# Two graph layers on one core: head and tail written in another order, filler matmuls at more places, and another address for one small tile

## The chip, the cores and the metric

The kernel runs on one core of a Trainium2 chip. The metric is the device time of one execution in microseconds (us), lower being better. The core has five engines that run side by side and wait for each other through semaphores: TensorE (PE in the profile; PEld is its loading of weights), VectorE (DVE), ScalarE (ACT), GpSimd (POOL) and SyncE (SP), which here only starts DMA transfers. The clock of TensorE can be granted in full or in part, and the profile shows which share it had.

## The reference

There are 128 graphs of 128 nodes with 512 features, and one adjacency matrix for each. Every graph goes through two layers, each of which normalises its input, applies relu, does a graph operation and adds the input back:

```python
h = jnp.maximum(_layernorm(x, axis=-1), 0.0)
x = x + _L0_gnn_ref(h, adj, W1, b1, gamma, beta, W2, b2)
h = jnp.maximum(_layernorm(x, axis=-1), 0.0)
x = x + _L1_gnn_ref(h, adj, W)
```

The first graph operation is a hypergraph convolution, relu, a layer norm over 1024 channels, a second convolution and a residual. The second takes the mean over neighbours and a linear layer of the features beside that mean:

```python
def hypergraph_conv(x, adj, W, b):
    H = (adj != 0).astype(x.dtype)
    w = adj.reshape(N, -1)[:, :C]
    xw = jnp.einsum('ncd,hd->nch', x, W)
    Dn = 1 / jnp.einsum('nce,ne->nc', H, w)
    Be = 1 / H.sum(axis=1)
    m = Be[:, :, None] * jnp.einsum('nce,nch->neh', H, xw)
    return Dn[:, :, None] * jnp.einsum('nce,neh->nch', H, m) + b
# layer 1
agg = jnp.einsum('bij,bjf->bif', adj, x) / jnp.maximum(deg, EPS)
out = relu(jnp.einsum('bnf,of->bno', jnp.concatenate([x, agg], 2), W))
```

## The kernel before

One tile is one graph: 128 nodes on the 128 partitions. The work on a graph is cut into some seventy small stages, each a Python function with the graph's number as argument (`x_sums`, `incidence`, `conv1_weights` and so on), and the order in which the stages are called is the order of the instructions on every engine. No planner chooses it: it is written by hand in three lists. `head` starts graphs 0 to 4 and prepares the weights, `step(s)` is repeated for s = 3 to 124 and holds stages of five or six graphs at different depths, and `tail` finishes the last seven, called y, z, a, b, c, d, e. A stage that was already called for a graph is skipped. `step` is not touched by the change.

Large products are done in a reduced-precision form of fp32 with both operands split into a high part h, a low part l and a combined part d. `product` (L440 to L463) runs h with h and l with l into one PSUM bank (L455; rm, gm, bm, am) and d with d into another (L460; rd, gd, bd, ad). So each weight needs three tiles: `Half.high` on ACT (L173), `Half.low` on DVE (L177), and `Half.rest`, which is one DVE operation (L189), four POOL operations (L80), or four matmuls with the tile `unit`, which holds two signed identities, and copies on ACT (L193 to L195, tile wd). Small products are full fp32: ps_s (L375, the node matrix s from the adjacency), pz (L413, features times s) and py (L628).

For one graph the stages run as follows.

- `load_adjb` brings the adjacency in 32 x 32 blocks (four DMAs of small pieces, two buffers), `incidence` turns and counts it on DVE (L361 to L369), `node_matrix` multiplies it and copies s on ACT (L377), and `node_scale` computes the scale dinv on DVE.
- `x_sums`, `x_spread`, `scales` and `x_norm` are the first norm: ACT sums with accumulators (L294 to L300), two small DVE operations (L305, L306), and ACT again (L310).
- `conv1_nodes` is pz, `conv1_high`, `conv1_low` and `conv1_rest` split it into z (ACT L426, DVE L430 and L433), `conv1_weights` is the product with one half of W1, `conv1_main` and `conv1_out` take it out of PSUM (ACT L475, DVE L480), and `conv1_bias` adds b1.
- `inner_sums` to `inner_norm` normalise the 1024 channels. `inner_out` and `inner_in` send r to DRAM and bring it back in blocks (n_scratch, nb, on SP), `inner_turn` turns the blocks on DVE (L516), and `inner_high`, `inner_low` and `inner_rest` make nh, nl and nd (L537, L80, L546).
- `conv2_weights` is the product gm/gd, `conv2_weights_out` and `conv2_bias` make g (L619, and L80 with the tile c), `conv2_nodes` is py, and `conv2_out` adds to x (L632). `residual` adds the first norm's output and b2 to x on POOL.
- The second layer has its own norm (`layer1_sums` to `layer1_norm`), trip through DRAM (h_scratch, hb), turn and split (hh, hl, hd), a product bm/bd whose result is split again (bh, bl, bd), and a product am/ad.
- `mean_operator`, `mean_out`, `mean_in`, `mean_transpose` and `mean_rest` divide the adjacency by its degree, turn it through DRAM (an_scratch, anb) and make the three parts `anp` (ACT L344, DVE L347 and L348). `aggregate` multiplies them with bh, bl and bd into the open banks am and ad (L710: three matmuls per graph), and `finish` writes the output.

Weights of these matmuls are loaded from the tile named last in a row such as `am<-bh,anp`: there anp is the loaded operand and bh the streamed one.

Two devices matter for the change. First, `fill(columns)` puts matmuls of a constant on the next PSUM bank that is asked for (L94), whose result nobody reads. In fp32 a filler of 512 columns is two matmul instructions, each 0.43 us at full clock and 0.85 at half clock in this trace. The last filler added to the list is issued first. Second, the address of a pool's tile follows from the order in which tags are first used: a tag that is first used later lies behind. `unit` (L202 to L209) borrows the tags anp and ant, so the call of `unit()` fixes the place of the mean operator's parts.

`load_w1`, `load_w2` and `load_w3` put large weight transfers on SP (256 or 512 KB each), `load_bias` a broadcast row, `load_affine` eight small transfers on POOL's queue, and `load_adjb(0, nc.scalar)` four transfers on ACT's queue. `beta_row(k)` (L256, tile pc) multiplies one row block of W2 with beta and reads w2's raw tile, which `scale_w2(k, engine)` then scales in place.

Of the kernel before, what the change touches and what calls it, by code (L numbers as in the profile page):

```python
# [24 lines left out]
def gnn_kernel(  # L25
# [31 lines left out]
    nc = tc.nc  # L57
# [338 lines left out]
    @stage  # L396
    def x_spread(g):
        spread((1, g), X[g], H0[g], D)
# [395 lines left out]
    def head():  # L794
        load_adjb(0, nc.scalar)
        load_w1(0, 0)
        copy(eps_root, eps, AF.Sqrt)
        w1[0].high(0)
        load_x(0)
        load_w1(0, 1)  # L800
        w1[0].low(0)
        x_sums(0)
        x_spread(0)
        load_w1(1, 0)
        fill(2816)
        w1[0].high(1)
        scales(0, 1)
        load_x(1)
        incidence(0)
        w1[0].low(1)  # L810
        unit()
        load_adjb(1)
        x_norm(0)
        w1[0].rest(0, nc.vector)
        node_matrix(0)
        conv1_nodes(0)
        load_w1(1, 1)
        incidence(1)
        x_sums(1, "A")
        load_w2(0)  # L820
        w1[1].high(0)
        load_affine()
        x_spread(1)
        scales(1, 1)
        conv1_high(0)
        node_matrix(1)
        conv1_low(0)
        conv1_rest(0)
        w1[1].high(1)
        w1[1].low(0)  # L830
        w1[0].rest(1, nc.gpsimd)
        conv1_weights(0, 0)
        node_scale(0)
        load_x(2)
        x_norm(1)
        load_bias(b2_bc, b2)
        load_adjb(2)
        conv1_nodes(1)
        beta_row(0)
        conv1_main(0, 0)  # L840
        beta_row(1)
        conv1_high(1, True)
        w1[1].low(1)
        residual(0)
        w1[1].rest(0, nc.vector)
        beta_row(2)
        conv1_low(1)
        beta_row(3)
        x_sums(2)
        scale_w2(1, nc.scalar)  # L850
        scale_w2(0, nc.scalar)
        w1[1].rest(1, nc.vector)
        x_spread(2)
        node_scale(1)
        load_bias(b1_bc, b1)
        conv1_out(0, 0)
        load_w2(1)
        scale_w2(3, nc.gpsimd)
        scales(2, 1)
        conv1_weights(0, 1)  # L860
        conv1_bias(0, 0)
        w2[0].high(0)
        conv1_rest(1)
        conv1_main(0, 1)
        conv1_out(0, 1)
        scale_w2(2, nc.scalar)
        x_norm(2)
        conv1_bias(0, 1, nc.vector)
        conv1_weights(1, 0)
        incidence(2)  # L870
        w2[0].high(1)
        inner_sums(0)
        load_adjb(3)
        beta_row(4)
        w2[0].low(1)
        load_w3(1)
        inner_spread(0)
        beta_row(5)
        residual(2)
        node_matrix(2)  # L880
        scale_w2(4, nc.scalar)
        beta_row(6)
        conv1_nodes(2)
        scales(0, 2)
        inner_norm(0)
        w2[0].rest(1)
        inner_out(0)
        w2[0].low(0)
        scale_w2(5, nc.gpsimd)
        beta_row(7)  # L890
        incidence(3)
        load_x(3)
        node_scale(2)
        w2[1].high(0)
        conv1_high(2)
        w2[0].rest(0)
        w2[1].low(0)
        conv1_low(2)
        conv1_main(1, 0)
        scale_w2(6, nc.scalar)  # L900
        scale_w2(7, nc.vector)
        conv1_weights(1, 1)
        residual(1)
        conv1_out(1, 0)
        conv1_main(1, 1)
        w2[1].high(1)
        conv1_rest(2)
        conv1_out(1, 1)
        w2[1].low(1)
        inner_in(0)  # L910
        conv1_bias(1, 1, nc.vector)
        x_sums(3)
        conv1_bias(1, 0)
        node_matrix(3)
        x_spread(3)
        inner_turn(0)
        load_w3(0)
        inner_sums(1)
        node_scale(3)
        conv1_weights(2, 1)  # L920
        inner_high(0)
        inner_spread(1)
        beta_out()
        inner_low(0, nc.vector)
        scales(1, 2)
        inner_norm(1)
        scales(3, 1)
        w2[1].rest(1, nc.gpsimd)
        inner_rest(0)
        w2[1].rest(0, nc.vector)  # L930
        conv1_weights(2, 0)
        w3[0].high(1)
        x_norm(3)
        residual(3)
        conv2_weights(0)
        w3[0].low(1)
        conv1_nodes(3)
        conv2_main(0)
        conv2_weights_out(0)
        load_x(4)  # L940
        w3[1].high(0)
        conv1_high(3, True)
        conv1_main(2, 0)
        conv2_bias(0, nc.vector)
        load_adjb(4)
        conv2_nodes(0)
        conv1_low(3)
        conv1_main(2, 1)
        w3[0].high(0)
        conv1_out(2, 0)  # L950
        inner_out(1)
        conv1_rest(3)
        inner_in(1)
        w3[1].high(1)
        conv2_out(0)
        load_adj(0)
        layer1_sums(0)
        incidence(4)
        layer1_spread(0)
        inner_turn(1)  # L960
        load_x(5)
        conv1_out(2, 1)
        inner_high(1)
        scales(0, 3)
        layer1_norm(0)
        conv1_bias(2, 1, nc.vector)
        conv1_bias(2, 0)
        inner_low(1, nc.vector)
        mean_operator(0)
        conv1_weights(3, 0)  # L970
        conv1_weights(3, 1)
        layer1_trip_out(0)
        inner_sums(2)
        inner_rest(1)
        inner_spread(2)
        mean_out(0)
        node_matrix(4)
        scales(2, 2)
        w3[1].low(0)
        inner_norm(2)  # L980
        layer1_trip_in(0)
        inner_out(2)
        mean_in(0)
        conv2_weights(1)
        w3[0].low(0)
        conv2_main(1)
        conv2_weights_out(1)
        conv2_bias(1, nc.vector)
        layer1_turn(0)
        w3[1].low(1)  # L990
        x_sums(4)
        x_spread(4)
        inner_in(2)
        w3[0].rest(1)
        scales(4, 1)
        layer1_high(0)
        layer1_low(0, nc.vector)
        load_adjb(5)
        conv2_nodes(1)
        w3[1].rest(0)  # L1000
        conv2_out(1)
        x_norm(4)
        w3[1].rest(1)
        mean_transpose(0)
        w3[0].rest(0, nc.gpsimd)
        node_scale(4)
        layer1_rest(0)
        load_adjb(6)
        load_adj(1)

    def tail():
        y, z, a, b, c, d, e = range(N - 7, N)
        conv2_bias(a)
        inner_out(b)
        conv1_main(c, 0)
        x_norm(d)
        layer1_high(z)
        conv1_out(c, 0)
        conv2_nodes(a)
        node_matrix(d)  # L1020
        mean_out(z)
        layer1_self_main(y)
        incidence(e)
        conv1_weights(c, 1)
        conv2_out(a)
        inner_in(b)
        inner_turn(b)
        layer1_low(z)
        layer1_rest(z)
        conv1_main(c, 1)  # L1030
        layer1_sums(a)
        layer1_self_out(y)
        conv1_out(c, 1)
        layer1_mean(z)
        layer1_spread(a)
        mean_in(z)
        layer1_mean_main(z)
        finish(y)
        scales(a, 3)
        residual(d)  # L1040
        conv1_nodes(d)
        conv1_bias(c, 0)
        inner_high(b)
        load_x(e)
        layer1_mean_out(z)
        conv1_bias(c, 1, nc.vector)
        conv1_high(d)
        layer1_mean_high(z)
        load_adj(a)
        inner_low(b, nc.vector)  # L1050
        layer1_norm(a)
        inner_rest(b)
        mean_operator(a)
        inner_sums(c)
        inner_spread(c)
        layer1_trip_out(a)
        layer1_self(z)
        scales(c, 2)
        layer1_trip_in(a)
        conv2_weights(b)  # L1060
        mean_transpose(z)
        conv2_main(b)
        conv1_low(d)
        layer1_mean_low(z)
        layer1_mean_rest(z)
        inner_norm(c)
        x_sums(e)
        node_scale(d)
        inner_out(c)
        mean_out(a)  # L1070
        mean_rest(z)
        conv1_rest(d)
        aggregate(z)
        x_spread(e)
        layer1_self_main(z)
        conv2_weights_out(b)
        conv1_weights(d, 0)
        inner_in(c)
        conv1_main(d, 0)
        layer1_turn(a)  # L1080
        layer1_self_out(z)
        layer1_high(a)
        node_matrix(e)
        conv2_bias(b)
        layer1_low(a)
        conv2_nodes(b)
        conv1_weights(d, 1)
        finish(z)
        scales(e, 1)
        conv2_out(b)  # L1090
        layer1_rest(a)
        conv1_main(d, 1)
        conv1_out(d, 0)
        layer1_mean(a)
        x_norm(e)
        layer1_sums(b)
        conv1_out(d, 1)
        conv1_nodes(e)
        conv1_bias(d, 0)
        mean_in(a)  # L1100
        inner_turn(c)
        load_adj(b)
        layer1_spread(b)
        layer1_mean_main(a)
        inner_high(c)
        conv1_bias(d, 1, nc.vector)
# [206 lines left out]
```

## Time and profile before

| | us |
|---|---|
| median of 3 runs | 2488.76 (2487.8 to 2488.9) |
| the profiled execution | 2490.09 |
| its span in the trace | 2488.2 |
| PE busy in the span | 2470.7 |
| from one aggregate to the next, in the steps (2338.52 to 2357.61) | 19.09 |
| first product of graph 0 starts | 14.95 |
| products of graph 1's second convolution (gm) start | 59.78 |
| last matmul starts | 2482.83 |

All durations come from one profiled execution. A row of the timeline gives the start and the length of a group of instructions on one engine in us, then the engine, the line, the operation and its tiles; matmuls overlap, so the spacing of their starts, not their length, is what a matmul costs PE. A row of windows gives, for a stretch of time, the busy us (and number of instructions) of PE, PEld, DVE, ACT and POOL, then the granted share of PE's clock, the busy share of the DMA engines and the GB/s that they moved. A row of waits names the waiting engine, tile and line, what released it, and the us in total, the number of waits and the longest.

### The profile page before, as it was taken

Reading aid. Unit: us, or ns where it says so; the run is one execution under the profiler, and the core shown is the slowest. Engines: PE = TensorE matmul, PEld = TensorE weight load, DVE = VectorE, ACT = ScalarE, POOL = GpSimd, SP = SyncE. Lnnn points to the kernel's source line nnn. Section 1 sums busy time; section 2 is a strip of 40 time slices with the busy share of each in tenths; the row PEclk is TensorE's granted clock in tenths of the full one; section 3 lists DMA queues with packets and bytes.
Section 4 is the critical chain, followed back from the end, with each engine's and each line's share of the span. In section 5 each row is a group of like instructions: output and inputs, shape, how many; then the busy total and the mean of one; then the engine's idle time right before and its main releaser. Section 6 shows DMA issues by size and latency. Waiting matters only on the chain.

```text
span 2488.2 us, 41066 instructions
## 1 busy us (share of the span) xinstructions
PE 2470.7 (99%) x11188; PEld 2005.9 (81%) x11188; DVE 1996.7 (80%) x4906; ACT 1940.8 (78%) x4125; POOL 1714.3 (69%) x2275
## 2 busy tenths in 40 slices
PE   8999999999999999999999999999999999999998
PEld 6788888888888888888888888888888888888886
DVE  7888787878788877887787778887878777878887
ACT  8877877787778777877787778778777877787775
POOL 5677767776777677767766776677677767776761
PEclk9999999999999999999999999999999999999999
DMA  7344333434443444344334433443334344334432
GB/s 184 113 130 127 120 123 125 130 119 129 126 123 120 128 127 123 119 129 132 122 118 129 130 121 120 130 127 121 124 126 127 121 129 128 121 120 129 131 113 92
DMA packets 408951, 311.35 MB, mean 125 GB/s; under 512 B 176656, under 2 KB 339984, under 8 KB 408720
## 3 DMA queue, kind: packets, MB, share of 16 engines
q1 hardware_dynamic: 407888, 308.66, 40.1%
q8 instruction: 88, 1.44, 0.3%
q14 instruction: 143, 1.17, 0.2%
q10 hardware_dynamic: 576, 0.07, 0.0%
q0 software_dynamic: 256, 0.01, 0.0%
HBM read 166.21 MB, written 142.34 MB: 124 GB/s over the span
## 4 chain that ended last, share of the span: by engine, by line
PE 96%; DMA 1%; DVE 1%; ACT 1%; issue 0%; SPq 0%; ACTq 0%; POOL 0%; DVEq 0%
PE rm L455 18%; PE gm L455 18%; PE am L455 9%; PE gd L460 9%; PE bm L455 9%; PE rd L460 9%; PE bd L460 5%; PE ad L460 5%; PE pz L413 4%; PE py L628 4%; PE am L710 2%; PE ad L710 1%; PE ps_s L375 1%; DMA b_bc<-in_b_dram 0%; DMA w21r<-in_w2t_dram 0%; DMA adjb<-in_adj_dram 0%
## 5 line engine op out<-in xcount | busy, mean ns | idle before, releaser
L80 POOL TENSOR_TENSOR g<-g,c 128x256 f32<-128x256 f32 x246 | 178.0, 744 | 633.4 <-DVE g L619 633.4
L80 POOL TENSOR_TENSOR r<-r,b_bc 128x256 f32<-128x256 f32 x500 | 361.3, 744 | 58.2 <-DVE r L480 39.1
L80 POOL TENSOR_TENSOR nl<-nt,nh 128x256 fp32r<-128x256 f32 x488 | 346.1, 742 | 0.0
L80 POOL TENSOR_TENSOR x_t<-x_t,b_bc 128x256 f32<-128x256 f32 x256 | 241.5, 963 | 2.3 <-DMA b_bc<-in_b_dram 2.3
L704 ACT ACTIVATE o<-am 128x512 f32<-128x512 f32 x127 | 76.2, 600 | 205.2 <-PE am L710 205.2
L80 POOL TENSOR_TENSOR hl<-ht,hh 128x256 fp32r<-128x256 f32 x248 | 231.0, 952 | 6.2 <-ACT hh L537 6.1
L294 ACT ACTIVATE h<-x_t 128x512 f32<-128x512 f32 x255 | 159.5, 626 | 96.3 <-DVE x_t L632 96.3
L480 DVE SCALAR_TENSOR_TENSOR r<-rd,dinv,r 128x512 f32<-128x512 f32 x256 | 190.6, 745 | 26.2 <-PE rd L460 26.2
L310 ACT ACTIVATE h<-x_t,st 128x512 f32<-128x512 f32 x255 | 205.1, 804 | 0.0
L683 DVE TENSOR_TENSOR gb_t<-bd,gb_t 128x512 f32<-128x512 f32 x127 | 87.9, 692 | 138.2 <-ACT gb_t L679 135.5
L632 DVE SCALAR_TENSOR_TENSOR x_t<-py,dinv,x_t 128x512 f32<-128x512 f32 x128 | 96.1, 751 | 122.7 <-PE py L628 122.6
L80 POOL TENSOR_TENSOR x_t<-x_t,h 128x256 f32<-128x256 f32 x256 | 184.1, 739 | 6.9 <-ACT h L310 6.9
L299 ACT ACTIVATE h<-x_t,st 128x512 f32<-128x512 f32 x255 | 183.0, 718 | 4.2
L475 ACT ACTIVATE r<-rm,dinv 128x512 f32<-128x512 f32 x256 | 173.4, 678 | 12.3 <-PE rm L455 11.9
L413 PEld LDWEIGHTS pz<-s,h 128*128 128x128 f32 x1024 | 134.0, 191 | 60.2 <-ACT s L377 41.9
L80 POOL TENSOR_TENSOR bl<-gb_t,bh 128x256 fp32r<-128x256 f32 x246 | 179.2, 752 | 1.8 <-PE am L455 1.8
L619 DVE TENSOR_TENSOR g<-gd,g 128x512 f32<-128x512 f32 x127 | 87.8, 692 | 94.6 <-PE gd L460 91.8
L310 ACT ACTIVATE r<-r,st 128x1024 f32<-128x1024 f32 x128 | 157.7, 1232 | 1.2 <-DVE st L306 1.2
L516 DVE STREAM_TRANSPOSE nt<-nb 128x1024 f32<-128x1024 f32 x127 | 156.1, 1229 | 0.2
L546 DVE SCALAR_TENSOR_TENSOR nd<-nh,nl 128x1024 fp32r<-128x1024 f32 x127 | 155.2, 1222 | 0.0
L721 DVE SCALAR_TENSOR_TENSOR o<-o,x_t 128x512 f32<-128x512 f32 x127 | 150.7, 1186 | 4.2
L455 PE MATMUL rm<-w11h,z 128*128 128x512 f32 x512 | 151.3, 417 | 0.0
(217 smaller groups left out, 7242.8 us busy)
## 6 DMA issues: line engine op xcount, KB each, us to landing
n_scratch<-r SPq DMA_DIRECT2D x128, 512.0 KB, 2.7
nb<-n_scratch SPq DMA_DIRECT2D x508, 128.0 KB, 2.8
x_t<-in_x_dram SPq DMA_DIRECT2D x128, 256.0 KB, 2.9
h_scratch<-h SPq DMA_DIRECT2D x127, 256.0 KB, 2.0
hb<-h_scratch SPq DMA_DIRECT2D x508, 64.0 KB, 2.0
out_dram<-o SPq DMA_DIRECT2D x127, 256.0 KB, 2.1
adj_t<-in_adj_dram SPq DMA_DIRECT2D x128, 64.0 KB, 1.9
an_scratch<-adj_t SPq DMA_DIRECT2D x128, 64.0 KB, 1.7
```

The source lines that it names most:

```text
L80: eng.tensor_tensor(dst[:, s], a[:, s], b[:, s], op)
L294: copy(junk, src, func, accum_out=t[:, 0:1])
L299: copy(junk, src, AF.Square, bias=t[:, 1:2], accum_out=t[:, 2:3])
L310: copy(dst, src, func, bias=t[:, 5:6], scale=t[:, 4:5])
L413: nc.tensor.matmul(z[:, k * P : (k + 1) * P], H0[g][:, k * P : (k + 1) * P], S[g], start=True, stop=True)
L455: nc.tensor.matmul(pm, left[i](k), right(i, k), start=(i == 0 and k == 0), stop=(i == 1 and k == kk - 1))
L460: nc.tensor.matmul(pd, left[2](k), right(2, k), start=(k == 0), stop=(k == kk - 1), skip_group_check=True)
L475: copy(R[g][:, HALVES[half]], PY.pop((g, half)), AF.Copy, scale=DN[g][:, 1:2])
L480: nc.vector.scalar_tensor_tensor(r, PR.pop((g, half)), dn[:, 0:1], r, MUL, ADD)
L516: nc.vector.transpose(nt.rearrange("p k (i b) -> p k i b", b=B), t.rearrange("p i k a -> p k i a"))
L546: nc.vector.scalar_tensor_tensor(t, h, 2.0**-12, low, MUL, SUB)
L721: nc.vector.scalar_tensor_tensor(o, o, 0.0, X.pop(g), MAX, ADD)
```

## The change

Only the lists in `head` and `tail` are rewritten. The set of stages is the same; what differs is their order, the fillers, and the engine of some elementwise stages. In the head the old list asks for one filler of 2816 columns ahead of the first matmul; the new one asks for 1152 and 1408 there, 768 after graph 0's pz, and further down 384, 128 and 896. `unit()` is called near the top, ahead of the first `incidence` and of the second `x_sums`, so that anp starts at byte 212,288 of a partition and not at 213,408; the buffers of x, adjb, h0, g, s, ant and the tile of the incidence move as well, while all the split weights and the tiles z, n and h keep their addresses. `w1[0].rest` of the first half goes from DVE to POOL and of the second from POOL to DVE, likewise `w2[1].rest`; some `scale_w2`, bias and low stages change their engine too. The calls of `step` are the same, line by line.

```diff
     def head():
+        load_x(0)
+        load_w1(0, 0)
         load_adjb(0, nc.scalar)
-        load_w1(0, 0)
+        load_affine()
+        x_sums(0)
+        unit()
         copy(eps_root, eps, AF.Sqrt)
+        x_spread(0)
+        scales(0, 1)
         w1[0].high(0)
-        load_x(0)
+        x_norm(0)
+        fill(1152)
+        load_x(1)
+        x_sums(1, "A")
         load_w1(0, 1)
         w1[0].low(0)
-        x_sums(0)
-        x_spread(0)
         load_w1(1, 0)
-        fill(2816)
+        incidence(0)
+        load_adjb(1)
         w1[0].high(1)
-        scales(0, 1)
-        load_x(1)
-        incidence(0)
+        load_w1(1, 1)
+        fill(1408)
         w1[0].low(1)
-        unit()
-        load_adjb(1)
-        x_norm(0)
-        w1[0].rest(0, nc.vector)
         node_matrix(0)
+        x_spread(1)
+        incidence(1)
         conv1_nodes(0)
-        load_w1(1, 1)
-        incidence(1)
-        x_sums(1, "A")
+        node_scale(0)
+        fill(768)
+        conv1_high(0)
+        scales(1, 1)
+        w1[0].rest(0, nc.gpsimd)
         load_w2(0)
...
+        conv2_main(0)
         x_norm(3)
+        fill(384)
+        w3[0].high(0)
+        conv2_weights_out(0)
+        conv2_bias(0, nc.vector)
+        conv1_nodes(3)
+        incidence(4)
+        fill(128)
...
+        load_adjb(6)
...
+        load_adjb(5)
...
+        inner_in(2)
+        load_adj(1)
+        fill(896)
         w3[0].rest(0, nc.gpsimd)
-        node_scale(4)
-        layer1_rest(0)
-        load_adjb(6)
-        load_adj(1)
 
     def tail():
...
+        conv2_weights_out(d)
+        layer1_turn(c)
+        layer1_high(c)
+        aggregate(b)
+        conv2_bias(d, nc.vector)
+        conv2_nodes(d)
+        layer1_low(c, nc.vector)
```

In the middle part of the head, which the excerpt leaves out, `load_adjb(2)` comes after `load_w2(1)` and not before `load_bias(b1_bc, b1)`; `scale_w2(5)` goes from POOL to ACT and stands ahead of `inner_norm(0)`; `w3[1].high(0)` comes ahead of `inner_norm(1)`, and `x_spread(4)` and `conv2_main(1)` ahead of `inner_norm(2)`.

## The prediction

> **What bounds the kernel now.** I read the page's busy times and slices first, then a table of windows, then the waits of TensorE (PE), then its timeline matmul by matmul.
>
> ```profile
> span 2488.2 us, 41066 instructions
> ...
> PE 2470.7 (99%) x11188; PEld 2005.9 (81%) x11188; DVE 1996.7 (80%) x4906; ACT 1940.8 (78%) x4125; POOL 1714.3 (69%) x2275
> ...
> PE   8999999999999999999999999999999999999998
> ...
> PE 96%; DMA 1%; DVE 1%; ACT 1%; issue 0%; SPq 0%; ACTq 0%; POOL 0%; DVEq 0%
> ```
>
> PE is busy all the time but in the first and last slice. The windows (PE busy is the second number, the granted clock the one after POOL) say where the rest lies:
>
> ```profile
> 0.00:10.00 10.00, 7.84 (x12) 3.28 (x12) 2.50 (x9) 6.12 (x11) 5.47 (x15) 1.00 0.71 223
> 15.00:20.00 5.00, 5.00 (x14) 3.98 (x14) 4.86 (x9) 2.62 (x4) 3.02 (x3) 0.50 1.09 248
> 60.00:80.00 20.00, 18.56 (x80) 13.63 (x79) 18.56 (x34) 18.56 (x41) 11.95 (x15) 1.00 0.36 109
> 80.00:100.00 20.00, 18.21 (x75) 14.08 (x74) 15.55 (x35) 14.97 (x33) 13.90 (x19) 0.91 0.39 120
> 200.00:1200.00 1000.00, 1000.00 (x4564) 816.11 (x4563) 802.35 (x1991) 783.67 (x1673) 709.38 (x943) 1.00 0.40 126
> 2450.00:2460.00 10.00, 8.79 (x35) 5.99 (x34) 7.26 (x16) 5.81 (x13) 0.00 (x0) 1.00 0.39 125
> 2460.00:2470.00 10.00, 8.35 (x35) 6.28 (x34) 8.26 (x18) 3.13 (x6) 2.63 (x4) 1.00 0.33 99
> ```
>
> From 100 to 2450 us nothing waits. Head and tail hold two kinds of loss, idle PE and a halved clock. The longest waits of PE in the head, and in the tail:
>
> ```profile
> PE ps_s L375 <- DVE sb L369: 1.8, 1, 1.8
> PE gd L460 <- DVE nd L546: 1.8, 1, 1.8
> ```
>
> ```profile
> PE py L628 <- POOL w11ds L80: 1.6, 1, 1.6
> ```
>
> The head's sum: up to rd of graph 4 (end 90.74 us) about 24.6 us are lost: 13.6 before the first product (14.95, less 1.3 of useful matmuls), 2.6 for its 12 matmuls at half clock (5.27 instead of 2.72), 1.9 around the waits for nh and g, 2.6 around the wd matmuls (65.35 to 72.40 takes 7.05, its work 4.5), and 3.9 at 80.7 to 90.7, where the wait for nd turns into a second cold stretch.
>
> The steady stage has a loss of its own, which busy time hides. One aggregate (L710, the matmuls with the mean operator's parts `anp`) and what stands around it:
>
> ```profile
> 2336.70 1.07 PE L460 MATMUL gd<-w20d,nd 128*128 128x512 f32 x4
> 2337.60 1.08 PE L460 MATMUL gd<-w21d,nd 128*128 128x512 f32 x4
> 2338.52 0.39 PE L710 MATMUL am<-bh,anp 128*128 128x512 f32 x1
> 2338.75 0.40 PE L710 MATMUL am<-bl,anp 128*128 128x512 f32 x1
> 2338.99 0.39 PE L710 MATMUL ad<-bd,anp 128*128 128x512 f32 x1
> 2339.22 1.09 PE L455 MATMUL rm<-w10h,z 128*128 128x512 f32 x4
> 2340.14 1.09 PE L455 MATMUL rm<-w10l,z 128*128 128x512 f32 x4
> 2341.07 1.07 PE L460 MATMUL rd<-w10d,z 128*128 128x512 f32 x4
> ```
>
> Starts are 0.2267 us apart inside a product (16 matmuls of gm take 3.63). From 2337.60 to 2341.07 there are 15 matmuls in 3.47, that is 0.2313 each: 0.07 too much, by the unrounded starts 0.067. It begins with the load of `anp` and takes some eight matmuls more to die out. The 48 loads of bm, am and gm, with bd, ad and gd, cost nothing; after the fp32 matmuls pz a shorter train (0.024) follows.
>
> **The Trainium skill.** TensorE: Matmul & The Clock Gate, section "What's actually happening": the clock is halved after an idle window of about 3.4 us and released after a busy one. The trace agrees: the half clock lasts from 13.5 to 20.3 us and from 85.2 to 88.6. The same page, "Step-by-step: what each phase is for", says that weights load ahead through a read port of their own; the 0.067 is not foreseen there. SBUF — State Buffer, "Operand start alignment", asks only for multiples of the element size and adds that its runs timed nothing, so on the speed of an address it is silent. ScalarE: Activation LUTs, "What ACT_TABLE_LOAD costs": about 1283 ns for a load; the trace has 1.28 at 2.74 us.
>
> **The change, part by part.**
>
> *Address of anp.* The buffer of the tag starts at byte 213,408 of a partition before (32 past a multiple of 64), at 212,288 after (a multiple). The steady steps' text is the same, so this is all that changes in them. For an effect: the excess starts exactly at these three loads, in every step, and the other reduced-precision operands all lie at multiples of 64. Waits don't explain it, since loads of hh, nl, nd also wait on semaphores and cost nothing. Against: fp32 operands at 32 past (two of the four s buffers; the h0 of graph 1, whose matmuls stand 0.112 apart like all others) show nothing, and unit, in the same buffer, was never seen loaded without a stall next to it. Upper end: all 0.067 x 124 steps = 8.3 us. Lower end: 0, or below: one of the four s buffers lengthens each fourth step by 0.02 (periods 19.09 instead of 19.07), so an address can also hurt. I take 8.3, since the kick has no other candidate.
>
> *Start of the head* (all durations are those of the timeline's rows of before). x comes first on SP, but x_sums now runs before the Sqrt of eps_root, and the built order has two table loads in place of one. ACT: table until 4.02, sums 1.0, second table 1.28, root 0.2, spread 1.2, w10h 1.05, so w10h stands at about 8.75 (before: 5.92). DVE: w10l 1.23, then incidence(0) from 10.0 to 11.55 (before 9.00 to 10.55; adjb(0) landed at 8.9 and goes on ACT's queue as before). ps_s at 11.6, s at 12.4, then ACT's x_spread(1) 1.2 and z-high 0.6: 14.2. The fillers ahead of ps_s shrink from 2816 to 2560 columns (0.43 less), all inside the wait, so free; the 768 after pz(0) take 1.3 warm, 2.6 cold, while incidence(1) runs to 14.3. ps_s(1) at 14.4 to 15.9. Then DVE has node_scale, scales, z-low, w10d (1.23, moved here from POOL), z-rest: 18.1. The product ends at about 19.1 instead of 20.2: -1.1. SP: eight transfers are out at a time, so w11, adjb(1) and w2 keep their places; adjb(2) moves behind w2(1), which so lands earlier (27.35 before), and adjb(2) still before its incidence at 29.6. The one wait added on SP is adjb(5), now behind adjb(6): it needs the buffer that incidence(4) frees at 54.4, and behind it are queued an_scratch and h_scratch of graph 0, not ready before 60: free.
>
> *Head to gm(0).* inner_norm(0) ends at 34.35 by the same sum (spread 31.5, two scale_w2 ahead of it, one of them moved there, 1.4, norm 1.25), before 34.41. The trip takes 2.9 + 4.5; DVE then is in the way (w20l, incidence(3), w21l twice, outs, bias) until 42.8, turn 1.23, and ACT has inner_sums(1) ahead of nh: gm(0) at 45.9, as before (45.85). The 1.1 is eaten by the wait for nh.
>
> *gm(0) to graph 4.* The fillers 384 and 128 (0.64 + 0.21) fit the time that g needs between gd and py (1.74 before, 0.9 of it pz): free. inner_norm(1) comes 0.8 later (w31h ahead of it), inner_norm(2) some 2 later (x_spread(4) and conv2_main(1) ahead). With the wd matmuls waiting for w31l and the filler of 896 (1.5), bm(0) starts at 73.9, not 72.4: +1.5. But nd(2) doesn't depend on PE: POOL's bias and nl (4 x 0.74), then scales behind inner_spread(3), give 84.0 (before 83.71). PE's wait shrinks from 1.8 to about 1.05, the window stays busy, and the second cold stretch (1.9) goes: rd of graph 4 ends at 89.3, not 90.7. Head: -1.4, with the ends -5 (no wait but the first) and +3 (a cold stretch of 3.4 us at half clock, 1.7, and a filler of 1.5 uncovered). nd(3) had 1.1 to spare (end 103.4, gd 104.54) and is next.
>
> *Tail.* PE's order is nearly the same. layer1_turn(c) now stands between g(d) and its bias: py(d) +0.6, but hh and hl no longer wait behind it (1.0 of bm): -0.35. The addition of c for graph e stays on POOL (2 x 0.73), so its wait of 1.65 stays. Swaps of DVE and POOL in low and bias steps (0.69 against 1.5) lie beside PE work with 20% and more of slack; uncovered, each costs 0.8. Ends -1.2, +1. After the last matmul nothing changes.
>
> Sum: -8.3 - 1.4 - 0.35 = -10.05. The profiled execution took 2490.09 (span 2488.2 and 1.89 around it), so 2480.0; it stood 1.33 above the median of the runs, 2488.76, so the median becomes 2478.7.
>
> **Rivals.** (1) The address does nothing, for which the fp32 operands speak; then 2488.76 - 1.75 = 2487.0, its own spread 2483.5 to 2490. (2) The new address is worse: 212,288 is 64 past a multiple of 128, while every other reduced-precision operand is at a multiple of 128. Place: each aggregate; price: another 0.067 x 124 = 8.3; it decides from 0.014 per step on (1.75 / 124). Time 2495.3. Against it speaks that the s buffer at 64 past shows no excess. (3) The address works and the head loses: its clock falls again while PE waits for nh: 2478.7 + 4.4 = 2483.1.
>
> **How the numbers follow.** Forecast 0.62, rival 1 0.25, rival 2 0.05, rival 3 0.08. Forecast alone: 2475 to 2482. About 0.2% (5 us) is what a measurement of this kernel can tell from no change; below 2483.8 lie the forecast, rival 3 in part and a little of rival 1: 0.70. Slower 0.06, same 0.24. The range 2475 to 2489 leaves out rival 2 and the ends of the others, some 0.15.
>
> **What would show it.** The address: from gd's last four to rd's first, 3.40 instead of 3.47, and periods of 19.00 to 19.02. The start: two table loads, rm near 14.5 to 16, no half clock near 85. If the period is still 19.07, step one is wrong; if gm(0) starts before 45, the head was under-rated; new waits between 100 and 2450 us would refute the claim that other engines have room.

## The result and the profile after

| | before | after |
|---|---|---|
| median of all runs, us | 2487.98 (18 runs, 2486.97 to 2488.9) | 2483.62 (18 runs, 2482.26 to 2485.61) |
| profiled execution, us | 2490.09 | 2483.95 |
| its span, us | 2488.24 | 2482.00 |
| aggregate of graph 2 starts, us | 125.44 | 123.53 |
| aggregate of graph 120 starts, us | 2376.69 | 2370.84 |

The ratio of the times is 0.9982, with a 95% interval of 0.9975 to 0.9988: 4.4 us less, where 10 were forecast. That is inside the range of 2475 to 2489, but outside the 2475 to 2482 of the forecast alone, and just short of the 0.2% that I called the bound of what a measurement can tell. The interval excludes no change all the same, so that bound was too wide.

The table splits the gain of the profiled execution. The head brings 125.44 - 123.53 = 1.91 us. The 118 steps between the two aggregates take 2251.25 us before and 2247.31 after, 3.94 less, or 0.033 a step. The rest, from 2376.69 and from 2370.84 to the end, is 0.39 shorter, of which the aggregates of three more graphs explain 0.10. Together 6.24, the difference of the spans. The medians differ by 4.4 only, because the profiled execution of before stood 2.1 above its median and that of after 0.3. More on that spread below.

The page of after, lines as shown of before: the first slice of PE shows a 9 now, and PE is busy 4.9 us less in all.

```profile
span 2482.0 us, 41095 instructions
...
PE 2465.8 (99%) x11200; PEld 2004.9 (81%) x11200; DVE 1998.6 (81%) x4905; ACT 1942.0 (78%) x4126; POOL 1717.0 (69%) x2282
...
PE   9999999999999999999999999999999999999998
```

The windows of after:

```profile
15.00:20.00 5.00, 3.99 (x20) 2.70 (x19) 4.90 (x10) 2.53 (x5) 2.48 (x3) 1.00 1.07 236
60.00:80.00 20.00, 18.17 (x78) 13.21 (x77) 16.67 (x32) 18.23 (x38) 13.30 (x17) 1.00 0.33 101
80.00:100.00 20.00, 20.00 (x93) 16.28 (x92) 15.23 (x38) 15.31 (x34) 13.51 (x19) 1.00 0.39 120
2450.00:2460.00 10.00, 10.00 (x46) 8.27 (x45) 9.22 (x21) 5.57 (x12) 0.00 (x0) 1.00 0.29 90
```

Between 80 and 100 us PE has neither a gap nor a slow clock (18.21 busy at 0.91 before), and between 15 and 20 the clock is 1.00 instead of 0.50. Between 60 and 80 us PE is idle for longer than before (18.17 busy instead of 18.56). The waits of PE up to 130 us in after, without those under 0.5 us and the 0.9 of the first filler:

```profile
PE ps_s L375 <- DVE sb L369: 2.9, 1, 2.9
PE wd L193 <- ACT w31d L195: 1.5, 1, 1.5
...
PE gd L460 <- DVE nd L546: 0.7, 1, 0.7
PE rd L460 <- DVE inv L385: 0.6, 1, 0.6
```

The wait for nd stays in the list, but it is another one: not graph 2 at 82, where gd now starts at 82.58 with nd finished at 82.40, but graph 3 at 102, whose nd ends at 102.45. In all it costs 1.0 us: the first two aggregates start at 84.42 and 104.48, 20.06 apart, where the steps have 19.04. The aggregate in the steps of after:

```profile
2331.84 1.07 PE L460 MATMUL gd<-w21d,nd 128*128 128x512 f32 x4
2332.74 0.40 PE L710 MATMUL am<-bh,anp 128*128 128x512 f32 x1
2332.98 0.39 PE L710 MATMUL am<-bl,anp 128*128 128x512 f32 x1
2333.21 0.40 PE L710 MATMUL ad<-bd,anp 128*128 128x512 f32 x1
...
2335.27 1.07 PE L460 MATMUL rd<-w10d,z 128*128 128x512 f32 x4
```

From the last four of gd to the first of rd it is 3.43 us, exactly between the 3.47 of before and the 3.40 that I expected. The steps were shortened, but by half.

### The profile page after: what moved, and what is told of

Same layout as the page of the kernel before. It is cut to its first block, busy times and chain, and to the rows that moved or that the text cites. A ratio compares the mean times of both kernels' runs of the same rounds, so it can differ in the third digit from the quotient of the medians.

```text
span 2482.0 us, 41095 instructions
## 1 busy us (share of the span) xinstructions
PE 2465.8 (99%) x11200; PEld 2004.9 (81%) x11200; DVE 1998.6 (81%) x4905; ACT 1942.0 (78%) x4126; POOL 1717.0 (69%) x2282
## 4 chain that ended last, share of the span: by engine, by line
PE 96%; ACT 1%; DMA 1%; DVE 1%; SPq 0%; issue 0%; POOL 0%; ACTq 0%; DVEq 0%
PE rm L455 18%; PE gm L455 18%; PE bm L455 9%; PE gd L460 9%; PE am L455 9%; PE rd L460 9%; PE bd L460 5%; PE ad L460 5%; PE pz L413 4%; PE py L628 4%; PE am L710 2%; PE ad L710 1%; PE ps_s L375 1%; DMA adjb<-in_adj_dram 0%; DMA n_scratch<-r 0%
## 5 line engine op out<-in xcount | busy, mean ns | idle before, releaser
L80 POOL TENSOR_TENSOR nl<-nt,nh 128x256 fp32r<-128x256 f32 x496 | 351.6, 741 | 6.0 <-ACT nh L537 6.0
```

The costliest lines, as they stand in the source:

```text
L80: eng.tensor_tensor(dst[:, s], a[:, s], b[:, s], op)
```

## The experiments

All are timed against the kernel before in the same way. "Excess" is the time of the fifteen matmuls from the last four of gd to the first of rd over 15 x 226.67 ns, from medians over the steps. "Period" is the mean distance of two aggregates.

| kernel | anp at byte | past a multiple of 256 | excess, ns | period, us | median, us | ratio to before, interval |
|---|---|---|---|---|---|---|
| before | 213,408 | 160 | 67 | 19.078 | 2488.0 to 2488.2 | |
| after | 212,288 | 64 | 33 | 19.045 | 2483.62 | 0.9975 to 0.9988 |
| e1 | 212,288 | 64 | 33 | 19.045 | 2483.82 | 0.9977 to 0.999 |
| e4 | 212,288 | 64 | 33 | 19.045 | 2484.34 | 0.9979 to 0.9992 |
| e2 | 212,896 | 160 | 67 | 19.098 | 2489.46 | 0.9998 to 1.0014 |
| e3 | 212,352 | 128 | 47 | 19.047 | 2482.90 | 0.9971 to 0.9988 |
| e5 | 212,224 | 0 | 0 | 19.012 | 2478.01 | 0.9949 to 0.9974 |
| e6 | 212,224 | 0 | 0 | 19.003 | 2478.06 | 0.995 to 0.9975 |
| e12 | 212,480 | 0 | 0 | 19.017 | 2478.94 | 0.9952 to 0.9977 |
| e13 | 212,224 | 0 | 0 | 19.012 | 2479.74 | 0.9955 to 0.998 |
| e7 | 212,288 | 64 | 33 | 19.045 | 2482.97 | 0.9972 to 0.9988 |
| e8 | 212,288 | 64 | 33 | 19.045 | 2481.51 | 0.9964 to 0.9984 |
| e9 | 212,288 | 64 | 33 | 19.045 | 2481.61 | 0.9965 to 0.9986 |
| e10 | 212,224 | 0 | 0 | 19.003 | 2477.10 | 0.9944 to 0.9969 |

An address is set by asking for tiles earlier, in the order in which they are to lie; nothing is computed with the tiles called "hold".

### Is it the address alone? (e1)

```diff
         x_sums(0)
+        pool.tile([P, 3, P], FP, tag="anp", name="hold")
         x_spread(0)
```

> The kernel before, with one tile of the tag anp asked for right after the first sums, so that anp starts at byte 212,288 as in the changed kernel; the order of all work is that of before, and the s buffers keep their places. Theory (the address alone shortens the steps): the distance from one aggregate to the next falls from 19.07 to 19.04 us, the time by 0.033 x 124 = 4.1, to about 2483.9. Rival (another buffer that moved with it, x, adjb, g or s, did it): distance stays 19.07, time 2488.

The order of before with the address of after has the excess of after to the nanosecond and 2483.82 us. Of the tiles that moved, only anp, adjt, sb and cnt did so here, and adjt kept its place against multiples of 256. The address of anp is the cause, and by the medians nearly all of the change's gain.

### The old address in the new order (e2), and a multiple of 128 (e3)

```diff
         x_sums(0)
+        pool.tile([P, P + 1], FP, tag="sb", name="hold")
+        pool.tile([P, 1], FP, tag="cnt", name="hold", bufs=2)
         unit()
```

> The changed kernel with anp at byte 212,896, that is 32 past a multiple of 128 as before the change; only small tiles and g move with it. Theory: the distance between aggregates goes back to 19.07 us and the time up by 4.1, to about 2487.7; the head keeps its gain of 1.9. Rival (the head's order did it all): 19.04 and 2483.6.

The excess is 67 again, so the first half of the reading holds. But the period is 19.098, longer than before's: adjt, which the fp32 matmul ps_s loads, moved too, to 160 past a multiple of 256, and now ps_s starts 235.0 ns after the matmul before it instead of 226.7, and the twelve matmuls after pz take 2.854 us with three of the four s buffers, where 2.837 was the rule. The place of a second loaded operand counts as well: sb, which ps_s streams, lies at 64 past a multiple of 256 as before. Of the twelve after pz this isn't shown, since g moved to 160 past a multiple of 256 together with adjt. By the period the steps cost 0.020 x 122 = 2.4 us more than before; the median is 1.3 above that of before, inside the interval, so the head gave some of it back.

The third kernel holds cnt alone ahead of `unit()`:

> The changed kernel with anp at byte 212,352, a multiple of 128 (the change put it at 64 past one). Theory A (whether a row of weights fills whole pieces of 128 bytes counts, and 64 past is half as bad as 32 past): the remaining 0.034 us of each aggregate goes, distance 19.00 to 19.01, time about 2479.5. Theory B (64 is enough, and the remaining 0.034 belongs to three lone loads in three banks, not to the address): 19.04 and 2483.6.

Neither theory was right: the excess rose from 33 to 47. A multiple of 128 is worse than 64 past it, so "fills whole pieces of 128 bytes" falls. The period hardly changed only because adjt, sb and g had moved to 128 past a multiple of 256 as well, which cost 10 ns at ps_s and gave 17 to 37 back after pz. What anp at 64, 128 and 160 have in common is that they differ from z, hh, nh and the weights, all 256 past a multiple of 512. That is the next theory.

### The tail alone (e4)

The kernel of e1 with `tail` of the changed kernel.

> The first of these kernels with the tail of the changed kernel. The tail by itself was put at -0.35 us: time 0.3 below the first one, which the runs can hardly show; the trace should, as the distance from the last steps' aggregate to the end. If the tail costs or gives more than 1 us, it shows in the time too.

From the aggregate of graph 123 to the end of the span it is 51.60 us in before and e1, 51.26 in e4 and 51.30 in after. By these traces the tail is worth 0.30 to 0.34 us; 0.35 was forecast. The other traces are less even: the old tail takes 51.55 in e13, the new one 51.16 to 51.40 in six more traces, but 51.54 in e3, 51.59 in e10 and 52.21 in e5. The times (2484.34 and 2483.82) can't tell it.

### The place of the neighbours (e5), all loaded tiles there (e6), a multiple of 512 (e12)

```diff
+        pool.tile([P, D], FP, tag="B", name="hold")
+        pool.tile([P, 3, P], FP, tag="anp", name="hold")
         x_sums(0)
         unit()
```

> The changed kernel with anp at byte 212,224, which is 256 past a multiple of 512 like every other operand of the split products (z, hh, nh, the weights); only the small sums tile changes places with it. So far the excess of one aggregate, against 226.7 ns for each matmul, was 67 ns at 416 past a multiple of 512, 33 at 320 and 47 at 384. Theory (an operand that lies like its neighbours costs nothing, any other place does): excess 0, distance between aggregates 19.007 instead of 19.040 us, time 4.1 below the changed kernel. Rival (33 ns belong to the three lone matmuls whatever the address): 19.040, no difference.

The excess is gone. One aggregate of this kernel:

```profile
2326.51 1.07 PE L460 MATMUL gd<-w21d,nd 128*128 128x512 f32 x4
2327.42 0.39 PE L710 MATMUL am<-bh,anp 128*128 128x512 f32 x1
2327.64 0.39 PE L710 MATMUL am<-bl,anp 128*128 128x512 f32 x1
2327.87 0.39 PE L710 MATMUL ad<-bd,anp 128*128 128x512 f32 x1
...
2329.91 1.07 PE L460 MATMUL rd<-w10d,z 128*128 128x512 f32 x4
```

That is 3.40 from gd to rd, and all three matmuls last 389 ns, where the medians of after are 398, 393 and 397. The whole 67 ns belonged to the address. The time, 2478.0, is 5.6 below after; the steps explain 0.033 x 122 = 4.1, and the rest is within the two intervals.

> As the one before, and the tiles ant, g, adjt and sb moved by 64 bytes too, so that adjt, which the fp32 matmul ps_s loads, also lies 256 past a multiple of 512 (320 in the changed kernel). Moving adjt to 384 cost 10 ns at ps_s and took 17 off the matmuls after pz. Theory (the loaded operand's place sets it): anp as in the run before, and another change of the matmuls from ps_s to the eighth after pz of up to -20 ns in each step, that is up to -2.5 us in all. Rival (only anp counts): the same time as the run before within 1 us.

Here the twelve matmuls after pz take 2.829, 2.829, 2.823 and 2.849 us, by which of the four s buffers is in use, instead of 2.837 (three times) and 2.857: 8 ns less a step on average, 1 us in all. The time shows no difference (2478.06). At ps_s adjt at a multiple of 256 costs 1 ns more than at 64 past one, which is next to nothing.

> The changed kernel with anp at byte 212,480, a multiple of 512 (the tiles behind it move by 192 bytes, the s buffers among them, so only the matmuls from the last four of gd to rd are read for the theory). Theory A (a multiple of 256 costs nothing): excess of the aggregate 0. Theory B (only the same place as the neighbours', 256 past a multiple of 512, costs nothing): an excess of 30 to 70 ns.

Here two small tiles of sums and the six of dinv are asked for ahead of anp. Theory A: the excess is 0 at a multiple of 512 too. It is not likeness to the neighbours; in these runs a multiple of 256 is enough.

### The order alone, at the free address (e13)

The edit of e5, made in the kernel before.

> The kernel before, with anp alone at byte 212,224 (256 past a multiple of 512) and the order of all work as before. The address alone should then give 0.067 x 122 = 8.2: distance between aggregates 19.007, time 2480.0. Set beside the same address in the changed kernel (2478.0) it gives what the new order of head and tail is worth: 2.0 by that sum, with -1.75 forecast. If the order is worth nothing: 2478.

2479.74 us, 8.3 below before: the 8.3 that my prediction had given to the address, by an address that the change doesn't reach. The new order at this address (e5) is another 1.7 lower, at the multiple of 512 (e12) 0.8, at 64 past (after beside e1) 0.2. All of these lie within the intervals.

### What holds the head? (e7, e8, e9, e10)

In `step`, for graph 4 alone:

```diff
+        if s == 4:
+            inner_rest(s - 1)
         scales(s, 2)
         inner_rest(s - 1)
```

> The changed kernel, where in the step of graph 4 alone DVE makes nd of graph 3 ahead of the two small operations that wait for ACT's sums of graph 4. Theory (nd of graph 3 is what is late after the head, 1.08 us in the profile of the changed kernel): no wait of gd near 102, the aggregate of graph 1 at about 103.4 instead of 104.5, time up to 1.1 lower. Rival (the next wait takes it, or the wait was not there in most executions): less than 0.4 of it in the time.

No wait for nd is left, and the aggregate of graph 1 starts at 102.69 instead of 104.48. But it starts at 102.70 in e2 and e3 as well, where nothing was done about nd, and none of e2, e3, e5 and e6 has a wait for nd. That wait belongs to the one execution of after. In time 0.65 was gained, more than the 0.4 that the rival allowed, but inside the interval; by the traces the rival holds.

The next kernel leaves out the line `fill(768)`, the one after it the lines `fill(384)`, `fill(128)` and `fill(896)`:

> The changed kernel without the filler of 768 columns behind the first pz. Theory (it lies beside DVE's incidence of graph 1, which ends at 13.8): the first product still starts at 14.3 to 15.9, but PE idles 1.3 us more there, and if its clock falls the product takes up to 2.6 us longer: rd ends between 18.6 and 21. The rest of the head waits for nh at 44, so the time stays within 0.5 us. Rival (the filler keeps the clock up and its loss is carried to the end): time +1 to +2.

> The changed kernel without the three later fillers (384, 128 and 896 columns). Theory (they are free or shield the clock): 384 and 128 lie beside the wait for g, no change at graph 0's pz; without 896, which takes 1.5 us ahead of the last pz before bm, bm of graph 0 starts 1.5 earlier (71.1 for 72.6), but gd of graph 2 then waits for nd, which does not depend on PE, so that 0 to 0.5 us is left in the time, and if the wait passes a window PE's clock halves near 85 (up to +1.7). Rival (nothing waits there): time -1.5.

Both are 2.0 to 2.1 us below after. Their intervals overlap with its, but the nine times of e8 (2480.90 to 2482.27) lie nearly all below the eighteen of after and the thirteen of e7 (2481.94 to 2485.34). Both theories missed that. In e8 the products up to gm of graph 1 are only 0.3 us earlier (58.22, 58.51 in e7). In e9 bm starts at 70.20, and as expected gd of graph 2 then waits for nd, while the clock stays full; its waits from 70 to 110 us, and its window:

```profile
PE gd L460 <- DVE nd L546: 1.3, 1, 1.3
```

```profile
80.00:100.00 20.00, 19.21 (x88) 15.72 (x89) 17.28 (x43) 16.62 (x35) 13.53 (x18) 1.00 0.43 128
```

Another 1.0 us came in both from a transfer. SP's queue in after, around graph 0's second trip through DRAM (h_scratch out, hb back):

```profile
59.05 0.35 SPq L501 DMA_DIRECT2D an_scratch<-adj_t  x1
59.51 0.36 SPq L501 DMA_DIRECT2D h_scratch<-h  x1
62.84 0.79 SPq L509 DMA_DIRECT2D hb<-h_scratch  x2
```

and in e9:

```profile
58.53 0.34 SPq L501 DMA_DIRECT2D an_scratch<-adj_t  x1
59.00 0.35 SPq L501 DMA_DIRECT2D h_scratch<-h  x1
61.15 1.12 SPq L509 DMA_DIRECT2D hb<-h_scratch  x2
```

The read waits for the write. From the issue of the write to that of the read it is 3.33 us in after and 2.15 in e9. In the order of before, h_scratch goes out ahead of an_scratch, and this takes 2.16 to 2.17 in all four traces of that order; in the new order 2.84 to 3.50 in the seven traces with all fillers, 2.14 to 2.27 in the three with some left out. After it stand the turn into ht, w31l, the wd matmuls and bm. So the new order loses about 1 us there that before didn't pay. An_scratch ahead of it suggests itself, but e8, e9 and e10 have it ahead too. The packets in the traces show another cause. The page of after has this line among the DMA queues:

```profile
q8 instruction: 88, 1.44, 0.3%
```

These are 88 transfers of 16,384 bytes of instructions, one for every 255 of PE's 11,200 matmuls and 11,200 loads, so they are taken to be PE's own. In all seven slow traces one of them (0.9 to 1.5 us long) begins before the first packet of the h_scratch write, and the write's last packets follow one another singly, as on one DMA engine that is behind; in after the transfer runs from 59.80 to 61.14 and the packets from 60.38 to 62.34. In all seven fast traces it begins when the write's packets are through or, in e8, at the last of them (60.90 in e9, packets from 59.85 to 60.68). The steps of after show the same: between 110 and 2380 us, eight h_scratch writes had such a transfer begin between 0.3 us ahead of their issue and 1.5 us after it, and landed after 2.86 to 3.32 us; the other 111 landed after 2.01 to 2.30. A filler is made of PE instructions, so leaving one out should let the next of these transfers come later, and it does: it begins at 60.31 in e8 and 60.90 in e9, at 59.23 in e7, with gm of graph 1 at 58.2 to 58.5 in all three. No run moved the transfer alone, so this rests on the traces.

The last kernel joins e6, e7 and e8:

> Three edits together: all of anp, ant, g, adjt and sb 256 past a multiple of 512 (2478.1 alone), no filler of 768 (-2.1 alone, of which the trace explained only 0.3 at the products and 1.2 by an earlier landing of graph 0's trip through DRAM), and nd of graph 3 first (-0.6 alone, within its interval). If they add up: 2475.4. If the filler's gain was the accident of a transfer: 2477 to 2478.

2477.10, in the band named for a gain that was the accident of a transfer. All five times are above 2475.4, though the interval reaches down to it. It is the lowest median of all, 0.9956 of before (0.9944 to 0.9969) and below the range of after, but not set apart from e5 and e6. Its trace still has 0.3 us of wait for nd and a clock of 0.66 between 10 and 20 us.

## Why the prediction was right or wrong, step by step

The time fell the way that was forecast, but the sum missed it by 4.9 us (2478.7 and 2483.62), and 4.2 of these are the address term. That the time lies in the range is in part luck: the range was made wide enough for two rivals. It lies beside rival 3's 2483.1, none of whose steps came true, since the address gave only half and the head did not lose; it even lies in the spread of rival 1, 2483.5 to 2490. What happened shows in the distance of the aggregates: 19.045 us, where before has 19.078 and the forecast said 19.00 to 19.02, half of the address gain.

*Address of anp: the right place, half the size.* Forecast -8.3, measured -3.94 over 118 steps, -4.1 over all 122 (I had counted 124). The reading of the kick was right: e5, e12 and e13 show that all 67 ns are the place of anp, and e1 that nothing else of the change touches the steps. What failed is the step from "32 past a multiple of 64" to "a multiple". I had compared anp with the other operands by their remainder to 64; by their remainder to 256 they are all 0, and after the change anp is at 64. Rival 2 saw that 212,288 is 64 past a multiple of 128, but only as a possible loss. Two sentences of mine were no evidence. I wrote that fp32 operands at 32 past a multiple of 64 "show nothing"; adjt at such a place (160 past a multiple of 256) costs 8 ns in e2. And I wrote "the s buffer at 64 past shows no excess"; but s is loaded only by the two long fp32 matmuls of py, not by one of reduced precision. The fourth step's 0.02, which I gave to one s buffer, is absent in e3 with the same s addresses: it hangs on the place of adjt or g as well.

*Start of the head: about right, and lucky in this execution.* The product of graph 0 ends at about 18.6, forecast 19.1, before 20.2. Two pieces came 0.35 to 0.45 early, and did so in every trace of the new head: w10h at 8.40 (8.75) and ps_s at 11.16 (11.6). The second ps_s, at 14.31 (forecast 14.4), had a full clock. In the six other traces of the new head with all fillers the clock between 10 and 20 us is 0.83 or 0.66, the second ps_s starts at 15.4 to 16.8 and the product ends at 18.7 to 20.1; in the three other traces of the old head it ends at 19.2 to 19.9. So the start gains some 0.5 on average, not 1.1. The second table load is there.

*Head to gm(0): wrong.* Forecast 45.9, measured 44.24. I let DVE stand in the way until 42.8. The row of DVE that decides it, in after:

```profile
41.08 0.68 DVE L80 TENSOR_TENSOR r<-r,b_bc 128x512 f32<-128x512 f32 x1
41.68 1.25 DVE L516 STREAM_TRANSPOSE nt<-nb 128x1024 f32<-128x1024 f32 x1
```

The bias ahead of the turn is nearly through when the last blocks land (41.5), so DVE delays the turn by 0.2 at most; ACT's sums of graph 1 and nh follow at once. inner_norm(0) had ended at 33.55, not 34.35. So the gain at the start was not eaten by the wait for nh; 1.6 were still there, and by the means of seven new and four old traces 1.2 (44.1 and 45.3).

*gm(0) to graph 4: the result nearly, by other parts.* bm(0) started at 73.38 (forecast 73.9): the fillers and the later trip cost what was gained, but 1.2 of that is the slow write, which was not in the sum. The nd of graph 2 was done at 82.40, not 84.0, so the wait went altogether, and the second cold stretch with it. That the wait causes the cold stretch, as I had it, is only half of it: e13 has the same wait of 1.8 us, and its clock stays full:

```profile
80.00:100.00 20.00, 18.21 (x83) 14.32 (x82) 15.94 (x39) 16.27 (x36) 15.25 (x21) 1.00 0.39 120
```

Three of the four traces of the old head have the cold stretch, so the forecast counted as certain a loss that comes in some executions. rd of graph 4 ends at 87.86 instead of 89.3. Then nd of graph 3, named as next, took 1.0 back in this execution. Head -1.9 instead of -1.4.

*Fillers: not shown to be free.* PE's clock between 80 and 100 us is full without the late ones too (e9), so they don't shield it there, and leaving out either group gave 2 us, though the intervals overlap; 1.0 of it is the shorter write. The 1.5 for 896 was in my sum as covered by nd of graph 2; in e9 that cover takes 1.3 of it back, and 0.9 still reaches the aggregate of graph 1 (101.78, 102.69 in e7).

*Tail: right in the traces of e4 and after.* -0.30 to -0.34, forecast -0.35; other traces of the new tail spread over 1 us. py(d) waits 1.47 instead of 0.96 us for g, +0.5 where +0.6 was forecast, and bm's wait for hl (0.16) is gone.

*The base of the sum.* I took the profiled execution's distance to the median of three runs, 1.33. With more runs it is 2.1. The aggregate of graph 1 shows how far executions differ: 103.83, 104.59, 104.67 and 106.36 in four traces of the old head, 102.69 to 104.48 in seven of the new with all fillers. By their means the head is worth 1.66, but two traces of one head differ by up to 2.5. The medians give 0.2 to 1.7 for head and tail together, so the 1.75 forecast for them is neither refuted nor shown.

## What to carry to other kernels

When matmuls of the same shape run back to back and a few of them are slower by some per cent, look at the start addresses of their loaded operands modulo 256 bytes, not only modulo the element or 64, and move the odd one: here 67 ns in each of some 122 steps, 8 us in all, for two lines that ask for a tile earlier. A change that reorders code can move addresses by the way, and then its gain belongs to the address; the old order at the new address is the experiment that tells. A head of 100 us, whose length differs by 2 us from execution to execution, is not judged by one trace of each. And when a transfer is late without other data on its way, look at the instruction queues too.

## What the runs showed of the hardware

- The loaded operand of a reduced-precision matmul (128 x 128, rows of 512 bytes) that starts at a multiple of 256 bytes cost nothing at the two addresses tried (e5, e12); three such loads at 64, 128 and 160 past one cost 33, 47 and 67 ns together. The loss is not in the three loads alone: in after six starts in a row come late (228 to 236 ns apart instead of 227), in before it runs over twelve, the later ones with well-placed operands. Why 128 is worse than 64, and by what mechanism an address costs time, was not settled.
- The loaded operand of the short fp32 matmul ps_s: next to no loss at 0 (1 ns, e6) and at 64 past a multiple of 256; at 128 (e3, where sb moved with it) and 160 (e2) the work up to pz comes 9 to 10 ns later. The twelve matmuls after pz change by -37 to +17 ns in these runs; whether by adjt or by g, which moved with it, was not told apart.
- The read behind the first 256 KB write of h could start 2.14 to 2.27 us after the write's issue in seven traces and 2.84 to 3.50 in seven others, with the same bytes, and a whole chain stood behind it. In the slow ones a transfer of 16 KB of instructions began ahead of the write's packets; in the fast ones it came behind them.
- With the same order of work in the head, TensorE's granted clock between 10 and 20 us was 1.00 in after, 0.83 in e2, e3, e5 and e7, and 0.66 in e6 and e12; with the old order it was 0.66 to 0.68. In the traces with 0.83 the half clock lasts for one stretch of 3.4 us (13.03 to 16.45 in e5), in those with 0.66 for 6.8 (10.81 to 17.64 in e6). It falls differently on the same instructions from run to run.
